# Six selective scans with the other layers' work between their tiles: summing two pairs late, slot ends where engines hand over, a larger carry, Newton steps on VectorE

## The chip, the cores and the metric

The kernel runs on one core of one Trainium2 chip. A core has five engines with an instruction stream each: TensorE (PE, matmuls), VectorE (DVE), ScalarE (ACT, activation functions), GpSimd (POOL) and SyncE (SP, which here issues the DMAs). The metric is the time of one execution on the device, in microseconds (us), as the median of several runs; lower is better.

## The reference

Four layers follow each other on x of shape 2 x 1024 x 256 (batch b, time, channels), each conditioned on a vector; all is float32.

- Layer 0: layer norm with a conditioned shift and scale, then a Mamba block: a projection to 512 channels twice (x and z), causal convolution over 4 steps, silu, a projection to a step size dt (softplus) and to B and C of 16 states, the selective scan, a gate silu(z), a projection back, a gated residual.
- Layer 1: two norms, projections to z and x, two such scans on convolved inputs, one running backwards in time, their sum gated by silu(x), a projection, a gated residual.
- Layer 2: linear attention (softmax of q over a head's channels, of k over time, a 16 x 16 product for each head), norm, conditioned scale and shift, silu, a projection, a residual.
- Layer 3: full softmax attention, 16 heads of 16 channels, 1024 x 1024, and the same closing.

The selective scan is the core, for each batch, for 512 channels and 16 states, over 1024 steps:

```
dA = exp(dt_t * A)
h  = h * dA + (dt_t * u_t) * B_t
y_t = sum over n of h[n] * C_t[n]   (+ u * D)
```

Layer 0 needs one scan for each batch (s00, s01), layer 1 two (s10 forward and s20 reversed; s11 and s21): six scans of 512 x 16 x 1024.

## The kernel before, in words

**Tiles.** A scan is cut into 64 tiles of 128 partitions x 1024 steps, each 32 channels x 4 states. Tiles go in pairs: for d in 0..3 (128 channels), cp in 0..1 (64 of them), k in 0..3 (states in fours), one pair, two tiles of 32 channels each. The four pairs of one (d, cp) make a group. 32 pairs a scan, 192 in all; `chain` (L991 to L1093) writes out their order by hand.

**One tile.** ACT computes the decay exp(dt * A) into PSUM, a ring of two (`decay`, L928). POOL multiplies dt*u with the spread B (`inputs`, L936) into a ring of eight tiles of SBUF (pool `hbp`, tag hb_t). DVE runs the scan instruction along time (`tile`, L947 forward, L943 reversed), then the product with C, on DVE (L950) or, for the first tile of a pair only, on POOL (L949): a "far" tile. Which it is, the program decides while it is built, from `lead`: a running account of estimated DVE work against POOL work. PE sums over states into a PSUM bank ys (`fold`, L974), after a first matmul with the diagonal matrix of D on u, and for the reversed scan with the identity on the other scan's y (`begin`, L960 to L964). The tile's ring slot comes free when PE has summed it. The fold of pair p - 1 is issued at the end of pair p. `finish` (L982, on DVE times the gate, or an ACT copy) takes a group's sum out two pairs after the group's end, in the pair with k = 2, and stores it.

**Loads.** All go through SP's queue in program order. A tile needs dt and dt*u spread over states (`load_spread`, L899; sp0 and sp1, rings of three), B and C spread over channels (`load_bc`, L889; eight tiles of one ring), and for each d the u, the y and a diagonal matrix (`load_rest`, L913), for each group the gate (`load_gate`). Stores are delayed by a number of slots (`save`, `later`).

**Other work.** Everything else while the scans run (projections of the next scans' inputs, norms, residuals, layer 2 and part of layer 3 for the first batch) is written as generators that stop at each `yield`. `Behind` (L804 to L870) queues them; `chain` calls `behind.slot(rates[i])` twice a pair, ahead of each tile's scan. A slot adds `rates[i]` columns to a credit (at most 2T = 2048, T = 1024) and room for ACT and POOL, and takes steps from the queue while the credit is positive and room is left. A step costs the PE columns it issued, at least a minimum, or what its yield says. A slot's work thus stands, on every engine, between two tiles of the scan. `pipe` (L365) makes the matmuls of the next bank before it takes out the last; its PSUM ring has two banks. Matmuls of all projections carry L95, transposes L99, activations L133.

**Norms.** `normed` (L438): DVE statistics (L394, L395), `root` on ACT (logarithm and exponential), `refine` (L405): one Newton step for the reciprocal root and the mean's product, seven small POOL operations in the scans (L410 to L416, tile newt) and four on DVE elsewhere; `scaled` applies both, on ACT (4 x 256 columns a tile) or in the tail on DVE. In layer 1's `first` the DVE and POOL (L141, `far_op`) scale and shift the normed block (the skip) before a second norm. `residual` (L786) adds a projection's bank to x on DVE (L791); `Closing` (L1533) schedules it after a scan's end.

**Stages.** Before the scans a prologue makes the first scan's inputs. After them comes the tail: layer 3's attention for both batches with layer 2 of the second behind it (scores L1418, maxima L1427, sums L1458).

Of the kernel before, what the change touches and what calls it, by code (L numbers as in the profile page):

```python
# [30 lines left out]
RATES = (2048, 2048, 1250, 1300, 1500, 1500)  # L31

LAG = 12

# [3 lines left out]
for _name, _n in (  # L38
    ("ln_g0", 2), ("ln_b0", 2), ("ada_b0", 4), ("conv_w", 16), ("conv_b", 4),
    ("dt_b0", 4), ("D0", 4), ("Alog0", 64),  # L40
    ("n2g", 2), ("n2b", 2), ("bx", 4), ("bz", 4), ("bc1", 4), ("bc2", 4),
    ("dt_b1", 4), ("dt_b2", 4), ("D1", 4), ("D2", 4), ("Alog1", 64), ("Alog2", 64),
    ("ng2", 2), ("nb2", 2), ("bk2", 2), ("bv2", 2), ("emb_b2", 4), ("fg2", 2), ("fb2", 2),
    ("ng3", 2), ("nb3", 2), ("bq3", 4), ("bk3", 4), ("emb_b3", 4), ("fg3", 2), ("fb3", 2),
    ("mask3", 16), ("bq3d", 2), ("bk3d", 2), ("ones3", 2),
):
    _COLS[_name] = (_NCOLS, _n)
    _NCOLS += _n
# [6 lines left out]
def kernel(ctx: ExitStack, tc: tile.TileContext, a: dict, out: bass.AP):  # L55
# [5 lines left out]
    hbp = ctx.enter_context(tc.tile_pool(name="hbp", bufs=8))  # L61
# [141 lines left out]
    nc.scalar.preload_act_table_set("natural_log_exp_and_others")  # L203
# [49 lines left out]
    def affine(mod, scale_at, shift_at, g, bias, name):  # L253

        s = const.tile([P, 2, B], F32, tag=f"{name}s", name=f"{name}s")
        o = const.tile([P, 2, B], F32, tag=f"{name}o", name=f"{name}o")
        for c in range(2):
            g_c, b_c = col(g, c), col(bias, c)
            at = mod[:, scale_at + c, :]
            act_f(s[:, c, :], at, AF.Identity, bias=g_c, scale=g_c)  # L260
            t = small_t((P, B), "aff")
            act_f(t, mod[:, shift_at + c, :], AF.Identity, bias=b_c)
            for b in range(B):
                act_f(
                    o[:, c, b : b + 1], at[:, b : b + 1], AF.Identity,
                    bias=t[:, b : b + 1], scale=b_c,
                )
        return s, o
# [34 lines left out]
    def cond_later():  # L303
# [7 lines left out]
        yield 5 * T  # L311
        made = []
        yield from pipe(*(
            cond_rows(w, scb, brow, i * D, b, f"{name}1_{b}", res)
            for b in range(B)
            for i, (name, res) in enumerate(
                (("shift", made), ("scale", made), ("gate", cond["gate1"]))
            )
        ))
        for b in range(B):  # L320
            o, s = made[2 * b : 2 * b + 2]
            t = small_t((P, 2, D), "t2", 1)[:, 0, :]
            nc.gpsimd.tensor_scalar(s, s, 1.0, None, ALU.add)
            nc.gpsimd.tensor_tensor(t, s, g1[:, 1, :], ALU.mult)
            nc.gpsimd.tensor_tensor(o, o, t, ALU.add)
            nc.gpsimd.tensor_tensor(s, s, g1[:, 0, :], ALU.mult)
            cond["s1"].append(s)
            cond["o1"].append(o)
            yield
# [75 lines left out]
    def refine(mv, r):  # L405

        q = small_t((P, mv.shape[1]), "newt", 2)
        e = nc.gpsimd if mode["scans"] else nc.vector
        if mode["scans"]:
            e.tensor_scalar(q, mv[:, :, 1], EPS, None, ALU.add)  # L410
            e.tensor_tensor(q, q, r, ALU.mult)
            e.tensor_tensor(q, q, r, ALU.mult)
            e.tensor_scalar(q, q, -0.5, 1.5, ALU.mult, ALU.add)
            e.tensor_tensor(r, r, q, ALU.mult)
            e.tensor_scalar(q, mv[:, :, 0], -1.0, None, ALU.mult)
            e.tensor_tensor(q, q, r, ALU.mult)  # L416
            spent["POOL"] += 900
            return q
        e.scalar_tensor_tensor(q, mv[:, :, 1], EPS, r, ALU.add, ALU.mult)
        e.scalar_tensor_tensor(q, q, -0.5, r, ALU.mult, ALU.mult)  # L420
        e.scalar_tensor_tensor(r, q, 1.5, r, ALU.add, ALU.mult)
        e.scalar_tensor_tensor(q, mv[:, :, 0], -1.0, r, ALU.mult, ALU.mult)
        return q

    def scaled(src, r, q):
        o = abuf((P, 4, D))
        for j in range(4 if mode["tail"] else 0):
            nc.vector.tensor_scalar(
                o[:, j, :], src[:, j, :], r[:, j : j + 1], q[:, j : j + 1], ALU.mult, ALU.add
            )  # L430
        for j in range(0 if mode["tail"] else 4):
# [6 lines left out]
    def normed(src, res):  # L438
# [6 lines left out]
        yield mode["least"] * 3 // 2  # L445
        q = refine(mv, r)
        yield
        for i, t in enumerate(src):
            res.append(scaled(t, r[:, ts(i, 4)], q[:, ts(i, 4)]))
            yield  # L450
# [7 lines left out]
    def channels(src, dst, func, scale, bias, halves=(0, 1)):  # L458
# [8 lines left out]
        def take(i, c, ps):  # L467
            act_f(
# [87 lines left out]
    def ssm_inputs(key, u, w_xp, w_dt, dt_b, st):  # L556
# [15 lines left out]
        if key == "00":  # L572
# [7 lines left out]
            take(0, pss[0])  # L580
            nc.vector.tensor_copy(dbl[:, 512:], pss[1][: R + 2 * N, :])
# [5 lines left out]
        save(2, st["bc"], dbl[R : R + 2 * N, :])  # L587

# [132 lines left out]
    def layer1(b, st1, st2):  # L721
# [16 lines left out]
        def first():  # L738
# [4 lines left out]
            yield from normed(xt, skip)  # L743
            for v in skip:
                nc.vector.tensor_tensor(v, v, twice(cond["s1"][b], 4), ALU.mult)
                far_op(v, v, twice(cond["o1"][b], 4), ALU.add)
                yield
            o = []
# [55 lines left out]
    class Behind:  # L804

        def __init__(self):
# [14 lines left out]
        def step(self):  # L823

            while self.queue or self.soon:
# [5 lines left out]
                try:  # L831
                    least = next(self.queue[0])
                    return max(work[0] - at, least or mode["least"])
# [4 lines left out]
        def slot(self, columns):  # L838
# [7 lines left out]
            self.credit = min(self.credit + columns, 2 * T)  # L846
# [29 lines left out]
    class Scan:  # L876
# [8 lines left out]
        def load_bc(self, k):  # L885
            for w in range(2):
                t = bcp.tile([P, T], F32, tag="bc", name="bc")
                at = w * N + k * NS
                nc.sync.dma_start(  # L889
                    t,  # L890
                    self.st["bc"][at : at + NS, :].unsqueeze(0).to_broadcast([DS, NS, T]),
                )
                self.bc[w][k] = t

        def load_spread(self, c, w):

            behind.until(lambda: len(self.st["have"]) > c // 4)
            t = spread.tile([P, T], F32, tag=f"sp{w}", name=f"sp{w}")
# [7 lines left out]
        def load_rest(self, d):  # L906
# [3 lines left out]
            self.rest[d] = {"D": diag(col(self.Dp, d), "dgD")}  # L910
            for key, src in srcs.items():
                t = fin.tile([P, T], F32, tag=f"f{key}", name=f"f{key}")
                nc.sync.dma_start(t, src[ts(d, P), :])  # L913
                self.rest[d][key] = t
# [5 lines left out]
        def load_gate(self, d, cp):  # L920
            if self.gate:
# [4 lines left out]
                self.rest[d]["g"] = t  # L926
# [7 lines left out]
        def inputs(self, c, k):  # L934
            e = hb()
            nc.gpsimd.tensor_tensor(e, self.sp[c, 1], self.bc[0][k], ALU.mult)  # L936
# [15 lines left out]
        def begin(self, d, cp):  # L952
# [3 lines left out]
            rest = self.rest[d]  # L956
            r = ts(cp, 64)
            for ch in range(2):
                o = self.ys[d, cp][ts(ch, 64), :]
                nc.tensor.matmul(  # L960
                    o, rest["D"][r, r], rest["u"][r, ts(ch, 512)], start=True, stop=False
                )
                if self.add is not None:
                    nc.tensor.matmul(  # L964
                        o, ident[r, r], rest["y"][r, ts(ch, 512)], start=False, stop=False
# [13 lines left out]
        def finish(self, d, cp):  # L979
            t = yp.tile([P, 512], F32, tag="y", name="y")  # L980
            if self.gate:
                nc.vector.tensor_tensor(t, self.ys[d, cp], self.rest[d]["g"], ALU.mult)  # L982
# [8 lines left out]
    def chain(scans, rates, early, mid, after):  # L991
# [29 lines left out]
        for w in range(2):  # L1021
            s.load_spread(0, w)
        s.load_bc(0)
        for w in range(2):
            s.load_spread(1, w)
        for k in range(1, NK):
            s.load_bc(k)
        s.load_rest(0)
        ahead(0, "decay")
        ahead(0, "inputs")  # L1030
# [5 lines left out]
        for p, (i, d, cp, k) in enumerate(pairs):  # L1036
# [10 lines left out]
            if k == 2 and cp == 1:  # L1047
                if d < 3:
                    s.load_rest(d + 1)
                elif nxt:  # L1050
                    nxt[0].load_rest(0)
# [25 lines left out]
            if k == 2 and nxt:  # L1077
                nxt[0].load_spread(nxt[1] + 1, 0)
# [7 lines left out]
            if final and i + 1 < len(scans):  # L1086
                scans[i + 1].load_bc(k)

            if p:
                fold(p - 1)  # L1090
        fold(len(pairs) - 1)
# [36 lines left out]
    def layer2(b, src, dst):  # L1128
# [11 lines left out]
        for c in range(2):  # L1140
# [14 lines left out]
            yield  # L1155
            sm = small_t((P, 1), "ksm")
            act_f(kT, kT, AF.Exp, bias=mx, accum_out=sm)
            yield
            yield
            nc.vector.reciprocal(sm, sm)  # L1160
            yield
# [42 lines left out]
        for t2 in range(NT // 2):  # L1204
# [15 lines left out]
            yield  # L1220
            act_f(q, q, AF.Exp)
            yield mode["least"] * 3 // 2
# [16 lines left out]
        at = small.tile([P, 2, P], F32, tag="at", name="at", bufs=1)  # L1239
# [158 lines left out]
    def attention(sts, done):  # L1398
# [24 lines left out]
        def top(n, step, j, ps):  # L1423
            t, ch = divmod(step, 2)
            if n not in mh:
                mh[n] = small.tile([P, NT, 2, 4], F32, tag="mh", name="mh", bufs=2)
# [88 lines left out]
    ctx.enter_context(tc.manual_schedule())  # L1515
    sts = [{"v": [], "qk": [], "y": []} for _ in range(B)]
    with ExitStack() as s:
        bcp, spread, fin, yp = [
            s.enter_context(tc.tile_pool(name=n, bufs=k))
            for n, k in (("bcp", 8), ("spread", 3), ("fin", 1), ("yp", 2))  # L1520
        ]
        psum.append(s.enter_context(tc.tile_pool(name="psS", bufs=1, space=bass.MemoryType.PSUM)))
        s00 = Scan("00", negA[0], "D0", False, True)
        s01 = Scan("01", negA[0], "D0", False, True)
# [70 lines left out]
        for _ in range(7):  # L1595
            behind.step()
        behind.add(
            cond_first(), cond_later(), p01, p10, p20, cond_last(), p11, p21,
# [12 lines left out]
    home[0] = ctx.enter_context(tc.tile_pool(name="act2", bufs=17))  # L1611
    psum.append(ctx.enter_context(tc.tile_pool(name="psA", bufs=1, space=bass.MemoryType.PSUM)))
# [11 lines left out]
def _layout(i):  # L1624
# [16 lines left out]

    def heads(v, const_at=None):
# [11 lines left out]
        "dt_b0": cols(f["L0_cond_dt_proj_b"]), "D0": cols(f["L0_cond_D_param"]),  # L1654
# [5 lines left out]
        "D1": cols(f["L1_cond_Dp1"]), "D2": cols(f["L1_cond_Dp2"]),  # L1660
# [59 lines left out]
```

## Time and profile before

| | |
|---|---|
| three runs | 2119.06, 2124.39, 2125.03 us; median 2124.39 |
| the profiled execution | 2117.43 us, its span 2115.4 us |
| busy, share of the span | PE 1626.8 us (77%), DVE 1745.5 (83%), ACT 1140.4 (54%), POOL 1356.9 (64%) |
| DVE scan instruction, 128 x 1024 | 2.287 us |
| product with C on DVE (L950) / on POOL (L949) | 1.225 us x285 / 2.381 us x99 |
| product with B on POOL (L936) | 2.399 us x384 |
| decay on ACT | 1.117 us x384 |
| idle time of PE ahead of fold matmuls (L974) | 153.5 us, of it 101.1 waiting for L949, 52.4 for L950 |
| idle time of POOL for a ring slot that a fold holds (L936 for ys L974) | 52.0 us in 20 waits |
| idle time of ACT ahead of decays for DVE's product (L950) | 432.8 us in 193 waits |
| loads, issue to landing | sp 512 KB 5.3 us, bc 512 KB 7.7, fu 512 KB 4.5, fg 128 KB 4.7 |

How to read it: the profile records one execution. "Busy" is the time in which an engine has an instruction of its own at work. An idle time is put down to the instruction whose end released the waiting one, "engine, tile, line". Idle time of an engine with less to do than others costs nothing in itself: ACT's 432.8 us are waits for a place in the ring of two decays, which DVE frees. Buffer numbers are left out of tile names: hb_t is any tile of the ring. The clock is what the throttle granted to PE, as a share of full speed. Time stretches are microseconds from the span's start.

### The profile page before, as it was taken

To read this page: it belongs to the slowest core of one execution; us is meant where nothing else is said; L and a number is where in the kernel's file an instruction comes from. 1 tells how busy PE (TensorE), PEld (TensorE's weight loads), DVE (VectorE), ACT (ScalarE), POOL (GpSimd) and SP (SyncE) were. 2 spreads that over 40 slices of the span, in tenths; PEclk is the share of its full clock that TensorE was granted. 3 is DMA by queue.
4 is the path that set the end of the run, shared out by engine and by line. 5 is a ranking of instruction groups with operands and counts; after the bars stand their busy time and mean duration, and the time that the engine had idled before them with its cause. 6 is when DMAs were issued, how large, how long until landed. Compare 5 with 4: busy or idle time off the path is not lost.

```text
span 2115.4 us, 22775 instructions
## 1 busy us (share of the span) xinstructions
PE 1626.8 (77%) x8112; PEld 617.7 (29%) x8112; DVE 1745.5 (83%) x1728; ACT 1140.4 (54%) x1583; POOL 1356.9 (64%) x667
## 2 busy tenths in 40 slices
PE   6576867288697547886945658944999899999997
PEld 3132313033141202222312323300545333333333
DVE  4688898898999999998999987998767757777763
ACT  5565666375546345764555453542044555656665
POOL 0789898898999999999998977998101211000000
PEclk9688968599796558988977865965899999999999
DMA  3663458245653555555653344332300111020001
GB/s 111 239 222 114 157 184 292 83 157 185 254 196 141 179 172 187 189 179 188 250 206 110 117 159 144 123 132 73 116 1 1 39 21 18 23 56 1 2 1 38
DMA packets 106870, 267.53 MB, mean 126 GB/s; under 512 B 14618, under 2 KB 39067, under 8 KB 106756
## 3 DMA queue, kind: packets, MB, share of 16 engines
q1 hardware_dynamic: 106756, 266.07, 37.1%
q8 instruction: 64, 1.05, 0.2%
q14 instruction: 50, 0.41, 0.1%
HBM read 195.90 MB, written 67.90 MB: 125 GB/s over the span
## 4 chain that ended last, share of the span: by engine, by line
PE 30%; DVE 10%; POOL 5%; issue 4%; ACT 2%; DMA 0%; DVEq 0%; ACTq 0%; POOLq 0%
PE sc_t L1418 13%; PE av_t L1458 6%; PE sc_t L95 4%; POOL hb_t L936 3%; PE bank_t L95 3%; DVE dA_t L943 2%; DVE mh L1427 2%; PE sc_t L99 2%; DVE dA_t L947 2%; POOL hb_t L949 1%; PE ys_t L974 1%; DVE hb_t L943 1%; ACT act_t L133 1%; POOL act_t L141 1%; DVE hb_t L947 1%
## 5 line engine op out<-in xcount | busy, mean ns | idle before, releaser
L936 POOL TENSOR_TENSOR hb_t<-sp,bc 128x1024 f32<-128x1024 f32 x384 | 908.8, 2399 | 88.5 <-PE ys_t L974 52.0
L133 ACT ACTIVATE dA_t<-sp,negA 128x1024 f32<-128x1024 f32 x384 | 428.5, 1117 | 548.3 <-DVE hb_t L950 432.8
L947 DVE TENSOR_TENSOR_SCAN dA_t<-dA_t,hb_t 128x1024 f32<-128x1024 f32 x195 | 445.9, 2287 | 62.3 <-ACT dA_t L133 35.1
L1427 DVE TENSOR_REDUCE mh<-sc_t 128x1 f32<-128x512 f32 x512 | 327.5, 686 | 110.2 <-PE sc_t L1418 109.8
L974 PE MATMUL ys_t<-hb_t,fold 128*32 128x512 f32 x1536 | 294.2, 781 | 153.5 <-POOL hb_t L949 101.1
L133 ACT ACTIVATE hb_t<-sc_t 128x512 f32<-128x512 f32 x512 | 276.9, 595 | 188.7 <-PE sc_t L1418 188.5
L950 DVE TENSOR_TENSOR hb_t<-dA_t,bc 128x1024 f32<-128x1024 f32 x285 | 349.1, 1225 | 21.4 <-DVE dA_t L947 0.5
L1418 PE MATMUL sc_t<-act_t 32*128 32x512 f32 x2048 | 336.6, 650 | 11.0 <-DVE mh L1427 7.3
L949 POOL TENSOR_TENSOR hb_t<-hb_t,bc 128x1024 f32<-128x1024 f32 x99 | 235.7, 2381 | 19.6 <-DVE hb_t L947 17.8
L784 POOL TENSOR_TENSOR act_t<-act_t,row 128x1024 f32<-128x1024 f32 x8 | 18.7, 2347 | 339.9 <-PE sc_t L99 193.3
L943 DVE TENSOR_TENSOR_SCAN dA_t<-dA_t,hb_t 128x1024 f32<-128x1024 f32 x90 | 205.7, 2285 | 9.2 <-POOL hb_t L936 6.0
L1458 PE MATMUL av_t<-hb_t,act_t 128*32 128x256 f32 x2048 | 164.3, 393 | 1.1 <-DVE act_t L1466 1.1
L95 PE MATMUL bank_t<-act_t,w_c_w 128*128 128x512 f32 x256 | 129.6, 657 | 41.2 <-ACT act_t L133 41.2
L133 ACT ACTIVATE act_t<-bank_t,cols 128x512 f32<-128x512 f32 (+1 forms) x206 | 129.9, 677 | 44.5 <-PE bank_t L95 38.7
L1418 PEld LDWEIGHTS sc_t<-act_t 32*128 32x128 f32 x2048 | 111.1, 185 | 120.9 <-issue 79.9
L974 PEld LDWEIGHTS ys_t<-hb_t,fold 128*32 128x32 f32 x1536 | 40.5, 123 | 358.9 <-POOL hb_t L949 139.5
L947 DVE TENSOR_TENSOR_SCAN hb_t<-dA_t,hb_t 128x1024 f32<-128x1024 f32 x61 | 139.0, 2279 | 3.9 <-ACT dA_t L133 3.6
L141 POOL TENSOR_TENSOR act_t<-act_t 128x1024 f32<-128x1024 f32 x50 | 118.4, 2367 | 0.2
L99 PE MATMUL bank_t<-ident,act_t 128*128 128x128 f32 x128 | 34.6, 426 | 92.5 <-ACT act_t L133 92.3
L95 PE MATMUL bank_t<-act_t,w_dt_w 64*128 64x512 f32 x96 | 74.6, 912 | 40.4 <-ACT act_t L133 34.4
L1458 PEld LDWEIGHTS av_t<-hb_t,act_t 128*32 128x32 f32 x2048 | 42.1, 108 | 190.5 <-issue 177.8
L1363 POOL MEMSET act_t<- 128x1024 f32 x8 | 7.6, 952 | 128.0 <-PE sc_t L1418 128.0
(176 smaller groups left out, 1833.9 us busy)
## 6 DMA issues: line engine op xcount, KB each, us to landing
sp<-dt SPq DMA_DIRECT2D x192, 512.0 KB, 5.3
dt<-act_t SPq DMA_DIRECT2D x48, 512.0 KB, 5.2
bc<-bc SPq DMA_DIRECT2D x48, 512.0 KB, 7.7
u<-act_t SPq DMA_DIRECT2D x24, 512.0 KB, 5.0
fu<-u SPq DMA_DIRECT2D x24, 512.0 KB, 4.5
y<-y SPq DMA_DIRECT2D x96, 128.0 KB, 5.8
g<-act_t SPq DMA_DIRECT2D x16, 512.0 KB, 5.3
fg<-g SPq DMA_DIRECT2D x64, 128.0 KB, 4.7
```

Source lines behind the costliest of these rows:

```text
L95: nc.tensor.matmul(o, w, x, **kw)
L133: nc.scalar.activation(o, x, func, **kw)
L141: nc.gpsimd.tensor_tensor(o, x, y, op)
L936: nc.gpsimd.tensor_tensor(e, self.sp[c, 1], self.bc[0][k], ALU.mult)
L943: nc.vector.tensor_tensor_scan(h[:, ::-1], dA[:, ::-1], e[:, ::-1], 0.0, ALU.mult, ALU.add)
L947: nc.vector.tensor_tensor_scan(h, dA, e, 0.0, ALU.mult, ALU.add)
L949: return lambda: nc.gpsimd.tensor_tensor(e, h, self.bc[1][k], ALU.mult)
L950: nc.vector.tensor_tensor(e, h, self.bc[1][k], ALU.mult)
L974: nc.tensor.matmul(self.ys[d, cp][at : at + DS, :], fold, e[:, ts(ch, 512)], start=False, stop=(k == NK - 1),)
L1418: nc.tensor.matmul(ps, w[r, ts(at, P)], x[r, ts(wide_at, 512)], start=True, stop=True)
L1427: nc.vector.tensor_reduce(mh[n][:, t, ch, j : j + 1], ps, AX.X, ALU.max)
L1458: nc.tensor.matmul(sums.av[32 * j : 32 * j + 32, ts(part, 256)], sts[b]["v"][t // 2][:, t % 2, 4 * g + j, :], es[j // 2][:, at : at + 256] ...
```

## The change

1. **Sums two pairs late.** `fold(p - 2)` instead of `fold(p - 1)` at the end of pair p; `hbp` has nine tiles instead of eight.
2. **Slot ends and carry.** A step may yield REST: its cost is taken from the credit, and the slot ends. It stands after the root and the refinement of a norm, after the first norm and the skip in layer 1, and in layer 2's softmaxes. The credit is capped at 4T instead of 2T, and the rates of scans 1, 2 and 3 change.
3. **Newton steps on VectorE** in the scans too, four operations for seven; the account of DVE's work gets 600 for it and 1800 for the skip.
4. **Loads.** sp0 has a ring of four and is loaded a pair earlier; B and C have rings of four each, the next scan's B loaded at the top of the pair; u, y and the diagonal of D come for each group of 64 channels, as two 64-partition DMAs, instead of for 128 channels.
5. **Prologue.** DVE takes half of the scaling, of the takes from PSUM, and the conditioned scale and shift; the first scan's first B is loaded right behind its store; the first input product is made on DVE.
6. **Layer 1's conditioning** is computed for each batch by itself, the second one later; two small tiles move to other pools.

```diff
-RATES = (2048, 2048, 1250, 1300, 1500, 1500)
+RATES = (2048, 2600, 1400, 1400, 1500, 1500)
+REST = -1
...
-    hbp = ctx.enter_context(tc.tile_pool(name="hbp", bufs=8))
+    hbp = ctx.enter_context(tc.tile_pool(name="hbp", bufs=9))
...
+            if not mode["scans"]:
+                t = small_t((P, B), "aff")
+                nc.vector.tensor_scalar(t, at, 1.0, None, ALU.add)
+                nc.vector.tensor_scalar(s[:, c, :], t, g_c, None, ALU.mult)
+                nc.vector.scalar_tensor_tensor(
+                    o[:, c, :], t, b_c, mod[:, shift_at + c, :], ALU.mult, ALU.add
+                )
+                continue
...
-        e = nc.gpsimd if mode["scans"] else nc.vector
...
-            spent["POOL"] += 900
...
+        nc.vector.scalar_tensor_tensor(q, mv[:, :, 1], EPS, r, ALU.add, ALU.mult)
+        nc.vector.scalar_tensor_tensor(q, q, -0.5, r, ALU.mult, ALU.mult)
+        nc.vector.scalar_tensor_tensor(r, q, 1.5, r, ALU.add, ALU.mult)
+        nc.vector.scalar_tensor_tensor(q, mv[:, :, 0], -1.0, r, ALU.mult, ALU.mult)
+        spent["DVE"] += 600
...
-    def scaled(src, r, q):
+    def scaled(src, r, q, i):
...
+        far = mode["tail"] or i and not mode["scans"]
...
         r = root(mv)
-        yield mode["least"] * 3 // 2
+        yield REST
         q = refine(mv, r)
-        yield
+        yield REST
...
+            if c and not (mode["scans"] or mode["tail"]):
+                nc.vector.tensor_scalar(
+                    dst[c][:, ts(i, 512)], ps, scale(c), bias(c), ALU.mult, ALU.add
+                )
+                return
...
+        if "first" in st:
+            later(2, st["first"])
...
             yield from normed(xt, skip)
+            yield REST
             for v in skip:
                 nc.vector.tensor_tensor(v, v, twice(cond["s1"][b], 4), ALU.mult)
+                spent["DVE"] += 1800
                 far_op(v, v, twice(cond["o1"][b], 4), ALU.add)
                 yield
+            yield REST
+            yield REST
...
                     least = next(self.queue[0])
+                    if least == REST and not mode["tail"]:
+                        self.credit -= max(work[0] - at, mode["least"])
+                        return 0
...
-            self.credit = min(self.credit + columns, 2 * T)
+            self.credit = min(self.credit + columns, 4 * T)
...
-            t = spread.tile([P, T], F32, tag=f"sp{w}", name=f"sp{w}")
+            t = spread.tile([P, T], F32, tag=f"sp{w}", name=f"sp{w}", bufs=4 - w)
...
+                rest[key] = t = fin.tile([P, 512], F32, tag=f"f{key}", name=f"f{key}")
+                for ch, half in enumerate(self.halves(src, d, cp)):
+                    nc.sync.dma_start(t[ts(ch, 64), :], half)
...
-        ahead(0, "inputs")
+        made["inputs"][0] = s.inputs(0, 0, nc.vector)
...
-            if k == 2 and cp == 1:
-                if d < 3:
-                    s.load_rest(d + 1)
-                elif nxt:
-                    nxt[0].load_rest(0)
+            if k == 1 and nxt:
+                nxt[0].load_spread(nxt[1] + 1, 0)
+            if final and i + 1 < len(scans):
+                scans[i + 1].load_bc(k, 0)
+            if k == 3 and nxt:
+                nxt[0].load_rest(nxt[1] // 4, nxt[1] // 2 % 2)
...
-            if k == 2 and nxt:
-                nxt[0].load_spread(nxt[1] + 1, 0)
...
-                scans[i + 1].load_bc(k)
-            if p:
-                fold(p - 1)
-        fold(len(pairs) - 1)
+                scans[i + 1].load_bc(k, 1)
+            if p > 1:
+                fold(p - 2)
+        for p in (2, 1):
+            fold(len(pairs) - p)
...
-            cond_first(), cond_later(), p01, p10, p20, cond_last(), p11, p21,
+            cond_first(), cond_later(0), p01, p10, p20, cond_later(1), cond_last(), p11, p21,
```

## The prediction

> **What bounds the kernel now.** I read the page first (busy shares, waits by group), then cut the span at the first scan instruction of each of the six selective scans and at the end of the last, and asked for each engine's busy time in every stretch. Columns: stretch and length in us, busy us (instructions) of PE, PE weight loads, DVE, ACT and POOL, granted clock, DMA share, GB/s.
>
> ```profile
> 0.00:69.50 69.50, 42.10 (x108) 21.56 (x108) 25.27 (x43) 34.98 (x51) 7.44 (x16) 0.87 0.42 149
> 69.50:310.00 240.50, 175.78 (x548) 60.79 (x548) 209.29 (x135) 159.53 (x196) 221.81 (x107) 0.80 0.50 171
> 310.00:561.00 251.00, 173.74 (x568) 61.08 (x568) 220.34 (x161) 149.95 (x174) 223.87 (x109) 0.83 0.54 184
> 561.00:791.50 230.50, 151.00 (x498) 53.17 (x498) 217.02 (x156) 112.61 (x145) 221.20 (x108) 0.67 0.54 190
> 791.50:1009.00 217.50, 172.64 (x540) 55.02 (x541) 206.58 (x121) 126.13 (x140) 208.91 (x91) 0.86 0.57 191
> 1009.00:1249.00 240.00, 153.00 (x627) 66.85 (x625) 228.15 (x181) 118.46 (x150) 211.97 (x98) 0.79 0.48 170
> 1249.00:1475.00 226.00, 150.56 (x512) 51.72 (x512) 200.76 (x132) 103.36 (x122) 207.97 (x109) 0.68 0.35 119
> 1475.00:2115.40 640.40, 608.00 (x4712) 247.46 (x4712) 438.12 (x805) 335.40 (x605) 53.76 (x34) 0.96 0.10 26
> ```
>
> Three regimes: a prologue of 69.5 us; six scans, 1405.5 us, with DVE and POOL busy 87 to 96% and nothing else near; a tail of 640.4 us that PE fills (608.0). The instructions of the tail stand in the same order in the changed kernel, so I give it 0. In the scans the time is the DVE's stream plus its stalls. DVE idles 31.2, 30.7, 13.5, 10.9, 11.9 and 25.2 us in the six, 123.4 together. Listing each stall gives 98.8 us, the rest being short gaps, and what the stalled instruction waited for sorts them. One from each of the larger sorts (start, duration, engine, line, work, idle before and its releaser):
>
> ```profile
> 182.34 4.05 ACT L133 ACTIVATE act_t<-act_t,newt,rstd 128x256 f32<-128x256 f32 x8 [3.52 <-POOL newt L416]
> 187.49 2.29 DVE L947 TENSOR_TENSOR_SCAN hb_t<-dA_t,hb_t 128x1024 f32<-128x1024 f32 x1 [3.58 <-ACT dA_t L133]
> ...
> 396.25 0.43 DVE L394 BATCH_NORM_STATS2 st<-act_t 128x6 f32<-128x256 f32 x1 [4.69 <-POOL act_t L141]
> ...
> 315.98 1.12 ACT L133 ACTIVATE dA_t<-sp,negA 128x1024 f32<-128x1024 f32 x1 [6.97 <-DMA sp<-dt]
> ...
> 506.98 0.69 ACT L133 ACTIVATE act_t<-bank_t,cols 128x512 f32<-128x512 f32 x1 [2.93 <-PE bank_t L95]
> ...
> 1273.54 0.69 DVE L791 TENSOR_TENSOR act_t<-act_t,bank_t 128x512 f32<-128x512 f32 x1 [7.86 <-PE bank_t L95]
> ```
>
> The first two are one stall: ACT stands 3.52 us for the seven small Newton operations, which are queued behind big products on POOL; its burst of 4.05 us comes late, the decay behind it too, and the scan waits 3.58. The third waits for a POOL addition, the fourth for a load whose ring was full, the fifth (ACT) for PE, which was handed more than it can do in a slot, and the sixth is a residual addition behind slow PE.
>
> **Normalisation: a step ends its slot (REST), Newton on DVE.** The stalls of the first sort are 3.58 (pair 15), 2.07 (42), 1.01 (92), 4.74 (142), 2.08 (160): 13.5 us. The change puts the slot's end between the root, the refinement and the scaling, and takes POOL out. Left is ACT's burst of 4.05 against the 2.29 + 1.23 = 3.52 us that DVE takes for a tile: 0.5 each, 2.7 in all. Gain 11. It isn't free: 8 norms of 4 DVE operations, with their spacing 0.8 each, add 6.4 to the bound engine. But the planner, which counts DVE's work, gives POOL 104 products with C where it gave 99, and 5 x 1.225 = 6.1 leaves DVE. These cancel. What is late next is the decay behind the burst.
>
> **Stats behind POOL in layer 1.** DVE stands 1.13 + 4.69 at pair 40 and 1.18 at pair 93, 7.0 us. One REST ahead of the skip and two behind it put slots between addition and stats. Gain 6.
>
> **POOL.** Newton leaves it, 56 operations in 8 sequences of 2.0 us (180.31 to 182.30 for one), -16; five products of 2.38 come, +12; the first input product goes to DVE, -2.4. Net -6 of 1296. Four groups of DVE stalls (pairs 2 to 4, 80 to 83, 121 and 122, 185: 14.1 us) come from POOL being behind. Between 0 and 14 I take 4, nearer to nothing, since POOL's load falls by half a per cent; POOL's waits for the bc loads (22.6 us in five) mostly sit beside other slack.
>
> **Rings.** dt's ring sp0 of four, loaded a slot and more earlier, takes away DVE's stalls behind late loads: 1.07 (pair 12), 2.36 (32), 2.21 (64), 5.6 us. Gain 5. The next scan's bc is loaded half a pair earlier on SP; the issue it now goes ahead of costs SP about 0.5 us, and the queue has room at a DMA share of 0.54.
>
> **Rest by quarters.** u and y of a group come as two 64-partition loads instead of a share of a 128-partition one; the diagonal tile is built 48 times instead of 24, ACT 24 x 0.39 = 9.4 us, beside 28 to 120 idle ACT us in each scan, +1. The Trainium skill, DMA: Bandwidth & Descriptors, Rules for kernel authors, speaks against it: two transfers to disjoint halves of the partitions share the same DMA engines, so one of 128 partitions is to be used. The rows: fg, already in such 128 KB halves, lands 4.7 us after issue, fu, a whole 512 KB, after 4.5. By rule and row the halves gain nothing. They'd cost if someone waited: they are issued a group ahead (three pairs, 21 us), so two loads of 4.7 one after the other, 9.4, are hidden. Were that cover gone, 48 groups x 0.2.
>
> **Folds two pairs late, hb ring of nine.** PE waits much for fold operands (153.5 us ahead of L974), and I give it no gain: by scan 3.7, 34.7, 41.7, 4.1, 12.6 and 56.6, it sits where PE has nothing else to do; at 500 to 515, where DVE stalls, PE is busy 15.00 of 15 us. In exchange the sums are a pair later and the ring only one tile longer: the second product of a pair needs the tile of fold p-3, now queued one pair closer; so does the gate (finish, L982), behind which the rest of DVE's pair is queued. PE's lag at the end of a pair is 2 to 4 us in the median. Of 32 DVE gates a quarter, late by 0.4, makes +3; below, -3 if queued folds now hold up PE less; above, +12 if POOL's product, whose lead over its scan is only 2.4 us in two scans, is often held.
>
> **Carry of four tiles, new rates.** I counted columns handed out per slot by the planner's own bookkeeping: slots over 3000 columns are 5 before and 13 after; in the second scan pairs 53 to 56 get 20480 columns in eight slots, before 16384. PE does 512 columns four times in 3.70 us, 1.8 ns a column, so 4096 columns are 7.4 us in a slot of 3.5. ACT empties the banks, and the next decay stands behind that. DVE has one tile in work and one decayed, 7.0 us, so the stall is 0 with full cover and 7.4 + 0.7 + 1.1 - 7.0 = 2.2 or more without. Stalls of this sort in the trace are 1.05, 0.91, 1.17, 1.02, 1.76 and 3.13, 3.93, 4.22, 4.43. For nine such slots I take 0.9 each, by the lower five, as most follow one or two slots that gave nothing or 1024: +8 (bounds 0 and 27).
>
> **Residuals.** The worst stall, 7.86 + 2.15 + 3.42 + 4.02 = 17.5 us at pairs 162 and 163, has no REST and nothing else in its way:
>
> ```profile
> 1267.00:1298.00 31.00, 30.75 (x76) 14.18 (x72) 14.66 (x18) 5.50 (x6) 17.46 (x8) 0.51 0.44 150
> ```
>
> PE is busy 30.75 of 31 us at half clock. The Trainium skill, TensorE: Matmul & The Clock Gate, What's actually happening, has the clock go to full after a busy window of about 3.4 us. By it the matmuls would run twice as fast in either kernel and the stall would be some 5. By the row the clock stays down through 30 busy us. I take the row, and 0: the planner puts the same steps within one or two pairs. A shift could free up to 12 or cost 6.
>
> **Prologue.** DVE takes four of eight scalings (0.442 each for 0.51 on ACT), half of the takes and the affine. ACT is 35 us busy of 69.5 and DVE 25. The second block's transposes, which wait 3.35 us for ACT now, start some 2.4 earlier. At its end
>
> ```profile
> 67.14 2.34 POOL L936 TENSOR_TENSOR hb_t<-sp,bc 128x1024 f32<-128x1024 f32 x1 [10.15 <-DMA bc<-bc]
> 69.51 2.30 DVE L947 TENSOR_TENSOR_SCAN dA_t<-dA_t,hb_t 128x1024 f32<-128x1024 f32 x1 [13.65 <-POOL hb_t L936]
> ```
>
> the first product waits for bc. The change issues that load behind its own store, and does the product on DVE (1.2 for 2.34). But some 3 MB go through at that point at 245 GB/s, and the second tile then waits for its spread. I take -2.8; together -5.2, bounds -3 and -7.
>
> **Sum.** -5.2 - 11 - 6 - 4 - 5 + 1 + 3 + 8 = -19.2 against the profiled execution's 2117.43: 2098.2. The median of the runs is 2124.39 / 2117.43 = 1.0033 of it: 2105.1. Its bounds: gains smaller and bursts dearer 2117, gains whole 2088.
>
> **Rivals.** One: the stalls have a common cause, the clash of steps in a slot, and with slot ends nearly all of them go, so that only the busiest engine counts. The third and fourth scan show it: POOL 221.2 of 230.5 and 208.9 of 217.5, 96%. The busiest engine's times, 221.8 + 223.9 + 221.2 + 208.9 + 228.2 + 208.0 = 1312.0, over 0.96 are 1366.7, 38.8 less than 1405.5; with the prologue 2073.4, as a median 2080. For it: two scans already do that. Against: PE-bound bursts and residuals, 45 us of stalls, get no remedy.
>
> Two, slower: the carry of four tiles. A slot that was ended early gives its credit to a later one, which pours 4096 columns on PE, and ACT's decay waits behind the takes, 4.5 us as at pairs 22, 24 and 57. Nine of these are 40 us against gains of 5.2 + 11 + 6 + 5 = 27: 2117.43 + 13 = 2130.4, as a median 2137. It decides once each costs more than 3 us. For it: the count of large slots, 13 for 5. Against: most follow slots with little in them, in which PE catches up.
>
> Three: nothing. Slot ends move the work a slot, where it meets the next burst, and the one-pair-shorter slack of the rings takes the rest: 2124, within 0.3% (6.4 us), about what a measurement of this kernel can tell from no change.
>
> **Numbers.** Forecast 2105.1, 0.42; rival one 2080, 0.23; two 2137, 0.21; three 2124, 0.14. Faster by over 0.3%: 0.65; same 0.14; slower 0.21. Leaving out the far tenth of each side, the range is 2062 to 2138; the gaining cases alone give 2068 to 2117.
>
> **What would show it.** Right: no ACT wait on newt, none of DVE's stats on POOL, few ACT waits for sp; first scan's start near 64; DVE idle in the scans near 105, most of the gain in the first, second and fifth scan; tail 640. Wrong: ACT waits for PE banks ahead of decays growing by tens of us (rival two), DVE idle down to 85 (rival one), or POOL's waits for ys far above 52.0 (folds dearer than 3).

## The result and the profile after

The changed kernel is slower: 2192.11 us in the median of four runs (2190.61 to 2198.08), the kernel before 2121.72 in four; ratio 1.0345, 95% interval 1.0312 to 1.0379. The profiled execution took 2198.08 us, its span is 2196.4.

The busy times by stretch, cut at the same places as before (first instruction of each scan, end of the last); columns as there:

```profile
0.00:66.40 66.40, 42.13 (x108) 21.26 (x108) 31.18 (x58) 29.44 (x37) 5.09 (x15) 0.88 0.44 155
66.40:321.50 255.10, 169.55 (x516) 60.24 (x517) 220.31 (x142) 166.42 (x205) 221.88 (x98) 0.76 0.51 170
321.50:581.20 259.70, 170.61 (x561) 60.37 (x561) 226.70 (x166) 146.11 (x174) 223.64 (x96) 0.81 0.52 178
581.20:824.40 243.20, 150.43 (x542) 57.31 (x540) 233.08 (x160) 109.87 (x143) 228.97 (x100) 0.70 0.52 180
824.40:1048.10 223.70, 170.38 (x546) 56.38 (x550) 207.38 (x123) 131.76 (x153) 208.04 (x89) 0.86 0.57 191
1048.10:1334.30 286.20, 168.62 (x650) 79.40 (x648) 242.57 (x188) 130.52 (x170) 216.66 (x93) 0.71 0.41 136
1334.30:1552.50 218.20, 126.91 (x488) 40.51 (x487) 204.49 (x134) 92.54 (x109) 204.45 (x94) 0.73 0.39 124
1552.50:2196.40 643.90, 610.94 (x4716) 248.60 (x4711) 436.99 (x806) 335.16 (x605) 53.60 (x33) 0.96 0.09 26
```

The prologue is 3.1 us shorter, the tail 3.5 longer; the scans take 1486.1 us for 1405.5. In them DVE's busy times add up to 1334.5 (1282.1 before, +52), its idle times to 151.6 (123.4, +28). Two things have grown, then, and busy time first: the mean durations of scans (2.29 us) and of products with C (1.22 us) haven't changed, so other DVE work must have.

It is the Newton steps. DVE and POOL rows of the timeline at the first norm:

```profile
168.35 1.23 DVE L965 TENSOR_TENSOR hb_t<-dA_t,bc 128x1024 f32<-128x1024 f32 x1
169.50 8.07 DVE L416 SCALAR_TENSOR_TENSOR newt<-mv,rstd 128x8 f32<-128x8 f32 x1
...
170.57 2.38 POOL L964 TENSOR_TENSOR hb_t<-hb_t,bc 128x1024 f32<-128x1024 f32 x1
172.87 4.68 POOL L951 TENSOR_TENSOR hb_t<-sp,bc 128x1024 f32<-128x1024 f32 x2
177.60 0.17 DVE L417 SCALAR_TENSOR_TENSOR newt<-newt,rstd 128x8 f32<-128x8 f32 x1
177.80 0.17 DVE L418 SCALAR_TENSOR_TENSOR rstd<-newt,rstd 128x8 f32<-128x8 f32 x1
178.00 0.17 DVE L419 SCALAR_TENSOR_TENSOR newt<-mv,rstd 128x8 f32<-128x8 f32 x1
178.09 2.28 DVE L962 TENSOR_TENSOR_SCAN hb_t<-dA_t,hb_t 128x1024 f32<-128x1024 f32 x1
```

An operation on 8 columns "takes" 8.07 us. It ends at 177.57, just after POOL's last product (177.55), and POOL then starts nothing for 2.9 us. So it outlasted the rest of one POOL product and three whole ones. In eight norms the first operation took 8.07, 0.15, 2.85, 8.62, 9.89, 7.76, 1.44 and 4.14 us, and 0.15 only where POOL stood idle. After each of the six that took over 2 us POOL had nothing to start for 2.9 to 6.4 us. The 32 operations are 49.1 us. (The first expectation below has 45.6 for the first ones; these add up to 42.9.) Layer 1's skip product of two SBUF tiles (L745 before, L752 after) went from 6.0 to 11.2 us in four.

The idle part is largest in the fifth scan: 43.6 us, before 11.8. The longest stall, at pair 133, and its causes:

```profile
1088.69 1.84 ACT L135 ACTIVATE act_t<-bank_t,cols 128x512 f32<-128x512 f32 x3 [9.37 <-POOL act_t L143]
1089.43 3.78 PE L97 MATMUL bank_t<-w_f_w,act_t 128*128 128x256 f32 x8 [15.12 <-ACT act_t L135]
...
1098.75 0.69 DVE L801 TENSOR_TENSOR act_t<-act_t,bank_t 128x512 f32<-128x512 f32 x1 [14.12 <-PE bank_t L97]
```
```profile
1084.00:1099.00 15.00, 9.56 (x22) 6.19 (x23) 0.88 (x2) 3.89 (x5) 9.39 (x4) 0.53 0.25 71
```

The slot, of 5120 columns by the planner's own bookkeeping, puts a projection and the residual's matmuls behind one another. ACT can't take the projection's bank until POOL is through with a tile; PE has no free bank and stands 15 us; then it runs at about half clock (0.53 in the row of these 15 us), and DVE's addition, with all of DVE's queue behind it, waits 14.12. Three waits for PE stand beside that one in the waits of the whole trace, total, times and longest:

```profile
POOL hb_t L951 <- PE ys_t L989: 103.6, 29, 16.6
DVE act_t L801 <- PE bank_t L97: 34.5, 10, 14.1
...
DVE y L997 <- PE ys_t L989: 12.1, 6, 5.7
DVE qmx L1228 <- PE bank_t L97: 11.7, 3, 5.8
```

The same four were 52.0, 24.5, 2.0 and 0.5 us (qmx: the maxima of layer 2's softmax). The sorts of stalls that the change aimed at did go: ACT's wait for newt fell from 14.5 us to 0.8, DVE's stats no longer wait for POOL (7.0), and ACT's waits for sp fell from 39.9 to 13.1. (POOL's waits for sp rose from 3.4 to 16.4, of which 12.2 is one wait at the first scan's start.)

### The profile page after: what moved, and what is told of

Its sections match the earlier page's. It is cut to its first block, busy times and chain, and to the rows that moved or that the text cites. A ratio compares the mean times of both kernels' runs of the same rounds, so it can differ in the third digit from the quotient of the medians.

```text
span 2196.4 us, 22940 instructions
## 1 busy us (share of the span) xinstructions
PE 1609.6 (73%) x8112; PEld 624.1 (28%) x8112; DVE 1802.7 (82%) x1769; ACT 1141.8 (52%) x1593; POOL 1362.3 (62%) x615
## 5 line engine op out<-in xcount | busy, mean ns | idle before, releaser
L951 POOL TENSOR_TENSOR hb_t<-sp,bc 128x1024 f32<-128x1024 f32 x383 | 918.0, 2438 | 153.5 <-PE ys_t L989 103.6
L962 DVE TENSOR_TENSOR_SCAN dA_t<-dA_t,hb_t 128x1024 f32<-128x1024 f32 x189 | 432.2, 2287 | 44.8 <-ACT dA_t L135 27.5
L989 PE MATMUL ys_t<-hb_t,fold 128*32 128x512 f32 x1536 | 268.1, 743 | 176.5 <-POOL hb_t L964 146.6
L965 DVE TENSOR_TENSOR hb_t<-dA_t,bc 128x1024 f32<-128x1024 f32 x280 | 342.8, 1224 | 20.8 <-PE ys_t L989 0.5
L1433 PE MATMUL sc_t<-act_t 32*128 32x512 f32 x2048 | 338.0, 656 | 11.8 <-DVE mh L1442 8.1
L964 POOL TENSOR_TENSOR hb_t<-hb_t,bc 128x1024 f32<-128x1024 f32 x104 | 247.7, 2382 | 33.8 <-DVE hb_t L962 24.5
L958 DVE TENSOR_TENSOR_SCAN dA_t<-dA_t,hb_t 128x1024 f32<-128x1024 f32 x91 | 208.1, 2286 | 16.1 <-POOL hb_t L951 9.9
L962 DVE TENSOR_TENSOR_SCAN hb_t<-dA_t,hb_t 128x1024 f32<-128x1024 f32 x67 | 152.7, 2279 | 6.0 <-ACT dA_t L135 6.0
L1433 PEld LDWEIGHTS sc_t<-act_t 32*128 32x128 f32 x2048 | 111.9, 186 | 121.3 <-issue 79.6
```

The costliest lines, as they stand in the source:

```text
L951: engine.tensor_tensor(e, self.sp[c, 1], self.bc[0][k], ALU.mult)
L958: nc.vector.tensor_tensor_scan(h[:, ::-1], dA[:, ::-1], e[:, ::-1], 0.0, ALU.mult, ALU.add)
L962: nc.vector.tensor_tensor_scan(h, dA, e, 0.0, ALU.mult, ALU.add)
L964: return lambda: nc.gpsimd.tensor_tensor(e, h, self.bc[1][k], ALU.mult)
L965: nc.vector.tensor_tensor(e, h, self.bc[1][k], ALU.mult)
L989: nc.tensor.matmul(self.ys[d, cp][at : at + DS, :], fold, e[:, ts(ch, 512)], start=False, stop=(k == NK - 1),)
```

## The experiments

Times are medians; a ratio is to the kernel before on the same chip, with its interval. Theory one, after reading the result: small DVE operations with two SBUF inputs wait for POOL. Its rival: slot ends and carry.

**newt_pool.** The seven POOL operations again:

```diff
-        nc.vector.scalar_tensor_tensor(q, mv[:, :, 1], EPS, r, ALU.add, ALU.mult)
...
+            nc.gpsimd.tensor_scalar(q, mv[:, :, 1], EPS, None, ALU.add)
...
+            spent["POOL"] += 900
```

> The changed kernel with only the Newton steps back on POOL (seven operations, their account as before). Theory one, the operands: a DVE operation with two SBUF inputs waits, inside its own duration, for POOL's running product and, where POOL has several queued, for the next ones too; the first Newton operation took 45.6 us in eight norms. Then this run is 35 to 50 us faster than the changed kernel, 2142 to 2157 us, and DVE's busy time in the scans falls by about 45. Theory two, the slots: DVE would have been stalled at these places anyway by slot ends and carry, and the long operations only hide stalls. Then the run is within 15 us of the changed kernel, 2177 to 2192.

2162.70 us, 1.0177 (1.0153 to 1.0201): 29 less than the changed kernel, between the two forecasts and nearer to theory one. DVE's busy time in the scans fell by 43.9 (1334.6 to 1290.7), but its idle time rose by 15.1 to 166.7. So part of the long operations did cover stalls.

**only_newt_dve.** The kernel before, with

```diff
-        e = nc.gpsimd if mode["scans"] else nc.vector
+        e = nc.vector
...
+        spent["DVE"] += 600
```

> The kernel before with only the Newton steps put on DVE in the scans. Theory one (two SBUF inputs wait for POOL): 25 to 45 us slower than before, 2147 to 2167, with first Newton operations of 2 to 10 us. Theory two (slots): within 8 us of before, 2114 to 2130, since nothing of slots and carry is in it.

2161.58 us, 1.0169 (1.0144 to 1.0195), +38: theory one. The 32 operations took 44.7 us, one of them 11.09, through five POOL products (the rest of one and four more); DVE's idle time stayed (121.3 for 123.4).

**newt_psum.** On DVE, with another operand:

```diff
+        ps = bank()
+        held[0] += 1
+        act_f(ps[:, :n], r, AF.Exp, scale=-0.5)
...
+            nc.vector.scalar_tensor_tensor(q, mv[:, :, 1], EPS, x, ALU.add, ALU.mult)
+            nc.vector.scalar_tensor_tensor(q, q, -0.5, x, ALU.mult, ALU.mult)
+            nc.vector.scalar_tensor_tensor(z, q, 1.5, x, ALU.add, ALU.mult)
+            nc.vector.scalar_tensor_tensor(q, mv[:, :, 0], -1.0, z, ALU.mult, ALU.mult)
+            nc.vector.tensor_copy(r, z)
+            held[0] -= 1
```

where x and z lie in ps.

> The changed kernel with the Newton steps still on DVE, one more of them (five for four), but the reciprocal root written by ACT to PSUM, so that each has one input in SBUF and one in PSUM. A bank of the ring of two is held for it over a slot. Theory one: the five take 0.2 us each, DVE busy falls by about 45, time 2145 to 2160. Theory two, or a wait that comes from DVE's place in the program and not from the operands: 2180 to 2195.

2159.89 us, 1.0167 (1.0141 to 1.0194), 32 less. The same place in its timeline, again beside POOL's products:

```profile
161.99 4.79 POOL L967 TENSOR_TENSOR hb_t<-sp,bc 128x1024 f32<-128x1024 f32 x2
...
166.25 0.15 DVE L424 SCALAR_TENSOR_TENSOR newt<-mv,bank_t 128x8 f32<-128x8 f32 x1
...
166.64 0.17 DVE L426 SCALAR_TENSOR_TENSOR bank_t<-newt,bank_t 128x8 f32<-128x8 f32 x1
166.68 2.40 POOL L980 TENSOR_TENSOR hb_t<-hb_t,bc 128x1024 f32<-128x1024 f32 x1
166.84 0.16 DVE L427 SCALAR_TENSOR_TENSOR newt<-mv,bank_t 128x8 f32<-128x8 f32 x1
166.93 0.16 DVE L428 COPY rstd<-bank_t 128x8 f32<-128x8 f32 x1
```

One input in PSUM, and the operation takes 0.14 to 0.17 us at each of the eight norms, POOL at work or not. That settles the operand, since engine and place are the same and there is one operation more.

**old_carry.** The changed kernel with

```diff
-            self.credit = min(self.credit + columns, 4 * T)
+            self.credit = min(self.credit + columns, 2 * T)
...
-RATES = (2048, 2600, 1400, 1400, 1500, 1500)
+RATES = (2048, 2048, 1250, 1300, 1500, 1500)
```

> The changed kernel with the cap of the credit at 2T and the rates as before. Theory one: it loses the 14.1 us stall at pair 133, where one slot hands out 5120 columns, and little else, 2172 to 2182. Theory two (slots and carry are the main cause): 40 us or more faster than the changed kernel, under 2152.

2153.79 us, 1.0131 (1.0108 to 1.0153), 38 less: about what the rival said, though Newton's operations still take 56.2 us here. Both theories hold, side by side. DVE's idle time fell from 151.6 to 114.1, in the fifth scan from 43.6 to 18.6. Of these 37.5 us, 34 are DVE's own waits for PE's banks, in the residual's additions and in layer 2's maxima (34.5 and 11.7 us in the changed kernel):

```profile
DVE act_t L801 <- PE bank_t L97: 6.7, 3, 2.9
...
DVE qmx L1228 <- PE bank_t L97: 5.5, 3, 2.5
```

The waits of DVE's scan instructions for a decay, the path on which the prediction put the carry's cost, were 44.2 us before, 38.0 in the changed kernel and 33.7 here: the carry had not made them longer.

**only_cap.** Only the first of old_carry's edits.

> The changed kernel with the cap at 2T and the new rates kept: it tells the cap from the rates. If the cap does the harm, it is near old_carry, 2150 to 2160; if the rates do (work comes earlier and the residuals meet other steps), near the changed kernel, 2182 to 2195.

2163.01 us, 1.0193 (1.0164 to 1.0222): 29 of the 38 are the cap's; the rates leave some 9. DVE's idle time is the same as in old_carry (114.7 for 114.1). By the traces, Newton's operations take longer (60.3 for 56.2 us), and the residual's additions wait 15.0 us for 6.7, which other waits make up for; so those 9 us aren't shown to be the rates' own.

**psum_carry.** newt_psum and old_carry together.

> Both causes taken away from the changed kernel: Newton on DVE with its root in PSUM, and the old cap and rates. If the two are separate (DVE busy longer in small operations; DVE idle behind slots of many columns) their gains of 33 and 39 us add up: 2112 to 2124. If they are two sides of one wait, the second brings little: 2140 to 2155.

2120.57 us, 0.9990 (0.9973 to 1.0006). They add up (32 + 38 of 72 us): two causes. Its time is that of the kernel before. (Its trace is of the fastest of 22 runs, 8 us under the median.)

**psum_carry_fold.** With it

```diff
-            if p > 1:
-                fold(p - 2)
-        for p in (2, 1):
-            fold(len(pairs) - p)
+            if p:
+                fold(p - 1)
+        fold(len(pairs) - 1)
```

> As psum_carry, with the sums one pair late again (the ring stays at nine). If the later sums cost what DVE's stalls in finish for ys show (10.1 us in the changed kernel, 19.2 with the old carry), it is 10 to 20 us faster than psum_carry, 2095 to 2112, and faster than the kernel before. If PE gains what the folds lose, it is within 4 us of psum_carry.

2114.60 us, 0.9958 (0.9944 to 0.9973): 6 less, under what was expected. DVE's stalls in finish went (16.0 us), but in the last scan the residual's additions waited more (5.4 to 19.1 us in all), with PE busy and at half clock:

```profile
1298.00:1330.00 32.00, 31.97 (x76) 14.60 (x80) 16.76 (x19) 7.72 (x7) 17.57 (x8) 0.52 0.29 94
```

**fold_early.** The same edit alone, on the changed kernel.

> The changed kernel with only the sums one pair late again, ring of nine kept. DVE's stalls in finish for ys, 10.1 us, go: 2180 to 2186. If the later sums help PE instead: 2192 to 2205.

2178.66 us, 1.0271 (1.0241 to 1.0302), 13 less. But Newton's operations also took 9 us less in this trace (40.0 for 49.1). The later sums cost 6 us where Newton is out of the way; more isn't shown.

**slot_2t.** newt_psum, with

```diff
-            while (self.queue or self.soon) and self.credit > 0:
+            left = self.credit - 2 * T
+            while (self.queue or self.soon) and self.credit > max(left, 0):
```

> newt_psum (new rates, credit capped at 4T) in which one slot hands out at most 2T of it and keeps the rest for the next. If the size of one slot's work is what the carry costs (more matmuls than a tile's time, at half clock after an empty stretch), it falls from 2160 to 2122 to 2138. If it is that the work comes earlier or in the same few slots one after the other, it stays at 2150 to 2162.

2157.61 us, 1.0165 (1.0138 to 1.0192): nothing gained. The size of a single slot isn't what the carry costs; the fifth scan's idle time fell by 16 us (43.7 to 28.0), and that of the others rose by 28.

**no_rest.** psum_carry_fold, with

```diff
-                        self.credit -= max(work[0] - at, mode["least"])
-                        return 0
+                        least = None
```

> psum_carry_fold, with a REST that doesn't end the slot (an ordinary yield in its place, in the scans). If the slot ends are worth what the prediction gave them (11 + 6 us): 2127 to 2135. If they only move the stalls: within 4 us of psum_carry_fold, 2110 to 2119.

2094.89 us, 0.9877 (0.9853 to 0.9901): 20 less, 17 by the ratios. Neither forecast: without slot ends the kernel is faster. The last scan of psum_carry_fold and then of no_rest shows all of it; the five ahead of it take 1171.6 us with slot ends and 1173.4 without:

```profile
1234.40:1471.80 237.40, 161.14 (x596) 62.38 (x596) 210.14 (x168) 107.27 (x134) 206.96 (x96) 0.74 0.38 120
```
```profile
1236.80:1455.10 218.30, 139.09 (x561) 52.84 (x560) 206.63 (x162) 104.75 (x130) 205.87 (x95) 0.77 0.41 131
```

In the last scan PE is busy 22 us longer with slot ends, and DVE idle 16 (27.2 for 11.7), 15.0 of its idle time in a residual's four additions: PE does it at half clock, the additions from 1305 to 1325, without slot ends within 12 us. But psum_carry, with slot ends too, also does it within 12 us. The stretch of the residual in psum_carry and then in no_rest, at full clock:

```profile
1303.00:1323.00 20.00, 19.93 (x94) 9.06 (x96) 16.75 (x20) 9.51 (x9) 18.68 (x8) 1.00 0.36 119
```
```profile
1280.00:1300.00 20.00, 18.05 (x80) 8.52 (x80) 17.57 (x21) 8.86 (x9) 20.00 (x9) 1.00 0.59 175
```

So this part hangs on the clock that the residual meets, not on slot ends alone. DVE's skip products, put at a slot's start with POOL's queue full, took 17.1 us for 8.5.

**cap_no_rest.** no_rest, with the cap at 4T.

> no_rest with the cap of the credit at 4T instead of 2T (rates old, one edit). If the cap does harm only where slot ends leave PE without work and the credit saved is then spent at half clock: within 6 us of no_rest, 2089 to 2101, and PE's empty stretches of over 3.4 us stay near 291 us in the scans. If a saved credit does harm by itself (more work than the time of the slots, whatever saved it): 2110 to 2135.

2111.75 us, 0.9921 (0.9893 to 0.9949), where before was 2129.06: by the ratios 0.4% (some 9 us) slower than no_rest, by the times 17. In the traces DVE's idle time is 17.5 us longer (115.2 for 97.7), and 13.1 of that is the residual's additions (20.3 for 7.2): PE does the last residual at half clock again (0.50 over 1255 to 1280, PE busy 25.00 of 25 us). So a larger cap costs without slot ends too, less than the 29 that it cost with them, and most of it through the residual. The expectation's count of PE's empty stretches hardly differs (297 us for 291; 422 in the changed kernel, 310 before).

**skip_psum.** psum_carry_fold, with

```diff
+            ps = bank()
+            held[0] += 1
+            for h in range(2):
+                mm(ps[:, ts(h, D)], ident, cond["s1"][b], start=True, stop=True)
             yield REST
             for v in skip:
-                nc.vector.tensor_tensor(v, v, twice(cond["s1"][b], 4), ALU.mult)
+                for h in range(2):
+                    nc.vector.tensor_tensor(
+                        v[:, ts(h, 2), :], v[:, ts(h, 2), :],
+                        ps.rearrange("p (t d) -> p t d", t=2), ALU.mult,
+                    )
```

> psum_carry_fold, with layer 1's skip multiplied by a scale that PE has spread into a PSUM bank, so that this DVE product too has only one input in SBUF (two halves of 512 columns for one of 1024; the bank is held over some slots). The four products took 17.1 us there and 6.0 in the kernel before. Operand theory: each half takes 0.7, 5.5 us in all, and the run is 6 to 12 us faster than psum_carry_fold, 2103 to 2109. If the wait isn't from the operands, the products still take 12 or more, and the time is 2111 to 2120.

2103.45 us, 0.9916 (0.9893 to 0.9939): 11 less; the operand again. The eight halves took 5.1 us, where the four products had taken 17.1.

**no_rest_skip.** Both.

> no_rest and skip_psum together: the four skip products took 8.5 us in no_rest, and should take 5.5 as halves with a PSUM input. 2086 to 2095, the fastest version here; if the bank held for the scale blocks other work, 2096 to 2104.

2087.03 us, 0.9806 (0.9777 to 0.9835), the fastest here, faster than both kernels. DVE's idle time in the scans is 90.8 us. Against skip_psum the five first scans are again the same (1163.9 and 1162.7 us), and the last is 15 us shorter.

**before_newt_psum.** The kernel before with newt_psum's edit.

> The kernel before with only the Newton steps on DVE, its root in PSUM (five operations of 0.2 us). By the operand theory the 38 us by which only_newt_dve was slower are gone; and if the prediction was right that leaving POOL frees the bursts of ACT behind Newton (11 us, less the operations' own 5), 2108 to 2118. If leaving POOL brings nothing: 2119 to 2127.

2108.14 us, 0.9934 (0.9900 to 0.9968), where before was 2129.06: 14 us faster by the ratio. Three of its nine runs lie 9 to 19 us above the median, the profiled one among them, so its trace isn't used. The time is as expected, if the operands are right. Which stalls went isn't shown.

## Why the prediction was wrong

**The step that failed first:** "8 norms of 4 DVE operations, with their spacing 0.8 each, add 6.4 to the bound engine." They took 49.1. The 0.8 for a norm fits the norms that the trace of before has on DVE (0.17 us for an operation), in the prologue and the tail, where POOL has little to do (busy 7.4 of 69.5 us and 53.8 of 640.4); in the scans it is busy 88 to 96%, as the first table of the prediction showed. The Trainium skill, SBUF — State Buffer, SBUF: two separate sides, says that a DVE operation with two SBUF inputs and a GpSimd operation that reads SBUF share a port pair that one holds for its whole instruction, while the other is blocked. An estimate by that rule: each first operation waits for up to one product of 2.4 us, 19 us in eight, which would have taken the forecast's gain of 19 away. The rows show more, 7.8 to 9.9 us in four of the eight, through three products or more, and 49.1 in all put the forecast on the slower side. The trace of before had the sign: one skip product (L745) with 2.22 us, where the others took 1.2 to 1.3.

**Newton off POOL:** the prediction gave 11 us to leaving POOL and slot ends together. In before_newt_psum leaving POOL alone gave 14 (7 to 21 by its interval), with another operand than the prediction had.

**Carry:** +8, bounds 0 and 27, was mis-sized: 29 for the cap, 38 with the rates. Its path was wrong too. Large slots were named, but the cost was put on ACT's decay behind the banks, so much for each large slot. slot_2t shows that it isn't the size of a slot, and the waits of scan instructions for decays did not grow (44.2 us before, 38.0 after); what grew is the waits of DVE's additions and maxima for PE's banks (25.0 before, 46.2 after, 12.2 in old_carry). Rival two's 2137 had the side right and, by itself, about the size (40), but by the same path; that its size fits is luck, and the measured loss has Newton in addition.

**Slot ends:** gains of 11 (with leaving POOL) and 6 were forecast. The stalls named did go, but the first five scans are no shorter with slot ends than without, and the last is 15 to 19 us longer. Between psum_carry_fold and no_rest, work moved by a slot met POOL's queue (8.6 us of skip products) and a residual at half clock (12). This is near to rival three's mechanism, which was given 0.14. That slot ends bring the half clock isn't shown: psum_carry and old_carry have them and full clock.

**Late sums:** +3 forecast, 6 measured (net of the slower residual in that trace), by the mechanism given: finish and POOL's inputs wait for a fold queued one pair later (2.0 to 12.1 us, 52.0 to 103.6; with the sums early again 18.0 to 2.0 and 55.7 to 6.3, from psum_carry to psum_carry_fold).

**Residuals** were put at 0, as a shift "could free up to 12 or cost 6". The reading of the row, a low clock in spite of a busy PE, held; the 0 didn't, for the clock changes with the order of the program. All of a trace's waits of the residual additions for PE, and the clock in the stretch of the last residual:

| trace | waits, us | clock, over |
|---|---|---|
| before | 24.5 | 0.51, 1267 to 1298 |
| changed kernel | 34.5 | 0.57, 1322 to 1346 |
| old_carry | 6.7 | 0.99, 1340 to 1360 |
| psum_carry | 5.4 | 1.00, 1303 to 1323 |
| psum_carry_fold | 19.1 | 0.52, 1298 to 1330 |
| no_rest | 7.2 | 1.00, 1280 to 1300 |
| cap_no_rest | 20.3 | 0.50, 1255 to 1280 |

**Right:** prologue -5.2 (-3.1 in the profiled execution, -6 in the fastest version), sp's ring by ACT's waits, the tail at nothing (+3.5, not explained).

In sum, in the order tested from the changed kernel: Newton's operand 32, carry and rates 39, late sums 6, no slot ends 20, skip operand 8 without slot ends (15 by the ratios); 105 us, down to 2087. The rest of the change (prologue, loads, the ring of nine, layer 1's conditioning) thus gains; by the ratios no_rest_skip is 41 us below before, of which Newton off POOL is 14 and the prologue 6. Which part gives the other 20 wasn't separated. Open is why the residual meets a low clock in one order of the program and full clock in another; no run changes that alone, and each row is of one execution. As it moves a result by some 12 us, differences of that size between two orders of the program need not be the edit's own; that holds for part of what is put down here to the carry and to slot ends.

## What to carry to other kernels

Before a small operation is moved to an engine, look at where its duration was measured and whether the other engines were as busy there; an operation's length can contain a wait that no wait row shows, so compare busy times, too. Beside a busy POOL, one input in PSUM instead of SBUF is worth a try for DVE's elementwise operations; here it took the wait from the Newton steps and the skip products. A stall that a change takes away is only a gain if the stretch gets shorter: test slot ends, carry and order each by themselves, and look at the clock in both traces before a difference is put down to the edit.

## What was not expected of the hardware

A DVE operation on 128 x 8 with two SBUF inputs took up to 12.88 us (in only_cap, through six back-to-back POOL products; 11.09 in only_newt_dve, through five), and mostly got through only when POOL ran out of work; in a few norms operations slipped in between two products (2.3 us each). The wait goes both ways: in the kernel before, four POOL products beside the skip products of DVE took 3.3 to 3.4 us for 2.38. A mask's scalar operation with one SBUF input (L1151) also took 4.41 us beside POOL's products; before it took 1.18, though POOL was at work then as well, so what decides there is open. bn_stats, with one SBUF input, didn't stretch in either kernel (112 in 44.8 and 44.7 us).

PE's clock stayed at half through long busy stretches: 0.51 with PE busy 30.75 of 31 us (before), 0.50 with 25.00 of 25 (cap_no_rest).
